# Layer 1's kept weights at the other end of SBUF, and SyncE's transfers of one pass in program order

## The chip, the cores and the metric

The kernel runs on one core of a Trainium2 chip. The metric is device time in microseconds: 1929.45 us before the change, the median of three runs (1929.41 to 1929.79). A core has five engines that run side by side [...]: TensorE (PE, matmuls), VectorE (DVE), ScalarE (ACT), GpSimd (POOL) and SyncE (SP). SyncE computes nothing here; it issues most of the transfers. GpSimd issues those whose rows are chosen by the data (indirect ones). [...]

## The reference, cut to what matters

Two layers, on 8192 tokens of 256 floats (128 graphs of 64 nodes). In each layer a graph part and then a part with experts is added to x:

```python
# layer 0
x = x + gnn0(layernorm(x), adj)          # silu(rmsnorm((adj @ h + eps*h) @ W1)) @ W2
x = x + ffn0(layernorm(x))               # 6 of 64 experts per token, each a 256x256 matrix, softmax weights;
                                         # the mix @ out_w, added to the input, layernorm (ln_g, ln_b)
# layer 1
x = x + gnn1(layernorm(x), adj)          # h = layernorm(.; gamma, beta); . + relu((adj @ h) @ W_rel + h @ W_root)
x = x + ffn1(layernorm(x))               # 2 of 8 experts per token: relu(x @ W1 + b1) @ W2 + b2, softmax weights
```

All of it is float32. The counts of tokens per expert are known only on the chip.

## The kernel before, in words

Tokens are worked on in NB = 32 blocks of C = 256 (T = 2 tiles of 128). There are four passes.

1. The first pass computes layer 0's graph part block by block, chooses six experts for each token, and has GpSimd scatter six copies of each row, with a destination row and a weight, into a table in DRAM that is sorted by expert (`r0x`; `Router.send`, L415).
2. The lattice pass (L1120 to L1222) reads that table in pages of 128 rows into `px` buffers, a ring of 31, multiplies each page by its expert's matrix in `lat` (128 KB of each partition of SBUF), weights the result in place, and has GpSimd scatter it back, one indirect transfer for each of 390 pages, into `r0y`, six rows per token (`Router.reply`, L424). At its end stands a branch (L1217) for pages that only an uneven choice of experts would need; it isn't taken in these runs. Where it isn't taken, each engine adds to the semaphores what its part of the branch would have added; GpSimd does so after waiting for all its earlier transfers.
3. The fused pass (L1348 to L1676) is the rest of layer 0 and layer 1's graph part and choice of experts. `load_y` (L1364) loads the six rows of each token of a block, `load3` (L1378) the residual x1 and the adjacency. `fold` (L1405, VectorE) adds two of the six rows to others from block 8 on, `mixture` (L1384) sums the rest with transposing matmuls, `out_proj` (L1396) applies out_w, `output` (L1414) the layernorm; `flip_h`, `neighbours`, `convolve_a` and `convolve_b` are layer 1's graph part with W_rel and W_root; `residual` (L1504) makes x3 and stores it; `flip3` (L1525) transposes it into `xn3T` by TensorE and a copy on ScalarE (L1529), and `gate1` (L1531) multiplies that by Wg. `choice`, `slots` and `send1` then place and scatter two copies of each row into a second table, `r1x`. Meanwhile `load_w2` (L1548) loads the eight W2 matrices of layer 1's experts into `fw2`, which is kept to the end.
4. The last pass works on pages of 256 rows of `r1x`: W1, relu, W2, and an accumulating scatter into the output. Its first four pages (-4 to -1) are fetched, and partly computed, in the fused pass's last stages (`fetch1`, L1252).

The order of the fused pass is written out by hand in the list at L1594: `staggered` runs stage s = -4, -3, -2 and so on, and an entry (lag, f) calls f for block s - lag. So in stage s there is load_y for block s + 4, load3 for s + 2, mixture for s + 2, out_proj for s + 1, output for s, the graph part for s - 1, residual, flip3 and gate1 for s - 2, choice, slots and the first row transfer for s - 3, and the rest of the rows and W2 for s - 4. Line 690 fixes this order on TensorE, VectorE and ScalarE. SyncE and GpSimd aren't in that list: a scheduler orders their instructions when the kernel is built.

Memory comes from pools. A pool is put at the lower end of what is free, or, with side="right", at the upper end. `lat` and above it `wx0`, with the `px` and `pxT` buffers, are freed before the fused pass; its pools then take the same bytes. With reuse_waits="tile" the first instruction that writes a tile waits for the last users of those earlier tiles whose bytes it takes, and for no others. In the kernel before, `keep` (fw2, 32 KB of each partition) takes the lower end of the old `lat`, then come `c3` (weights, adjacency) and `work3` (y, x1, xs, xn3T and the rest); `wx1` (layer 1's pages and W1) is at the upper end. `work3` ends at byte 174080; `lat` had ended at 154592, so that its last tiles (three of the four xs buffers and part of another, xn3T, the one-hot tiles) lie where pxT and px buffers were.

SyncE's transfers use eight completion semaphores in turn, so that at most eight are on their way: each waits for the one eight before it.

Of the kernel before, what the change touches and what calls it, by code (L numbers as in the profile page):

```python
# [9 lines left out]
F32 = mybir.dt.float32  # L10
# [3 lines left out]
ENG = mybir.EngineType  # L14
# [5 lines left out]
P = 128  # L20
# [637 lines left out]
def staggered(n, stages, first=0):  # L658

    for s in range(first + min(lag for lag, _ in stages), n + max(lag for lag, _ in stages)):  # L660
        for lag, f in stages:
            if first <= s - lag < n:
                f(s - lag)
# [3 lines left out]
def two_layer_gnn_moe_kernel(ctx: ExitStack, tc: tile.TileContext, a: dict, out: bass.AP):  # L667
    nc = tc.nc
    x_in, adjT = a["x"], a["adjT"]
    N, D = x_in.shape  # L670
# [3 lines left out]
    KD = D // P  # L674
# [7 lines left out]
    E1, F1, _ = a["L1_ffn_W2"].shape  # L682
# [34 lines left out]
    def load_matrix(pool, name, engine=nc.scalar):  # L717

        t = pool.tile([P, a[name].shape[0] // P, a[name].shape[1]], F32, name="m_" + name)
        engine.dma_start(out=t, in_=a[name].rearrange("(k p) f -> p k f", p=P))  # L720
        return t
# [20 lines left out]
    def clear_adjacency(pool, engine):  # L742
        for i in range(4):
            at = pool.tile([P, T, P], F32, name=f"at{i}")
            engine.memset(at, 0.0)
            adjacency.append(at)
# [31 lines left out]
    with tc.tile_pool(name="c0", bufs=1) as c0, \  # L778
# [290 lines left out]
        n = free[0] // 16  # L1069
# [153 lines left out]
    lat_pool.__exit__(None, None, None)  # L1223


    keep = ctx.enter_context(tc.tile_pool(name="keep", bufs=1, reuse_waits="tile"))
    fw1 = a["L1_ffn_W1b1"]
    F1W = fw1.shape[2]
    fw2 = keep.tile([P, E1, KF, D], F32, name="fw2")
# [66 lines left out]
    def bend(i, c0):  # L1296
        Q = pages[i]
        m = Q["n"] * P
        if c0 == 0:
            Q["hid"] = wx.tile([P, KF, PG], F32, name="phid")  # L1300
        for c in range(c0, c0 + Q["group"]):
            nc.scalar.activation(Q["hid"][:, c, :m], Q["up", c][:, :m], AF.Relu,  # L1302
                                 bias=Q["w"][:, KD * F1 + c:KD * F1 + c + 1], scale=1.0)

    def up(i):
        for c in range(0, KF, pages[i]["group"]):
            products(i, c)
            bend(i, c)
# [23 lines left out]
    def gather(i):  # L1332
        Q = pages[i]
        y, n = Q["x"], Q["n"]
        nc.vector.tensor_add(y[:, :n, :D], Q["py"][:, :n, :], Q["b2"].unsqueeze(1).to_broadcast([P, n, D]))  # L1335
# [12 lines left out]
    with tc.tile_pool(name="c3", bufs=1, reuse_waits="tile") as c3, \  # L1348
# [1 line left out]
            tc.tile_pool(name="ps3", bufs=3, space=PSUM, reuse_waits="tile") as psum, \  # L1350
            tc.tile_pool(name="po3", bufs=1, space=PSUM, reuse_waits="tile") as po_pool, \
            tc.tile_pool(name="pm3", bufs=1, space=PSUM, reuse_waits="tile") as pmix:
        out_wT = load_matrix(c3, "L0_ffn_out_wT")
        ln_g, ln_b, gamma, beta, bg = (over[x] for x in ("ln_g", "ln_b", "gamma", "beta", "bg"))
        w_rel, w_root = (c3.tile([P, KD, D], F32, name="m_" + x) for x in ("rel", "root"))
        wg = load_matrix(c3, "L1_ffn_Wg")
        clear_adjacency(c3, nc.vector)
        one = c3.tile([P, P], F32, name="one")
        nc.vector.memset(one, 1.0)
# [11 lines left out]
                    tc.declare_no_dep(d.ins, group="r0last", reason="in the first pages, or waited for above")  # L1371

        def load_weights(b):
            if b == 0:
                for t, v in ((w_rel, "L1_gnn_W_rel"), (w_root, "L1_gnn_W_root")):
                    nc.sync.dma_start(out=t, in_=a[v].rearrange("(k p) f -> p k f", p=P))

        def load3(b):  # L1378
# [90 lines left out]
        def flip_h(b):  # L1469

            B = blocks[b]
            pt = psum.tile([P, KD, C], F32, name="ps")
            ops.transpose(pt, B["hn"])
            B["hT"] = hT = work.tile([P, KD, C], F32, name="hT", bufs=1)
            for k in range(KD):
                nc.scalar.activation(hT[:, k, :], pt[:, k, :], AF.Identity, bias=beta[:, k:k + 1], scale=gamma[:, k:k + 1])
# [95 lines left out]
        def places_of(i):  # L1572
            def half(c):
                if c % 2 == 0:
                    pages[i]["two"] = (po_pool.tile([P, T, D], F32, name="po") if c % 4 == 2 else
                                       psum.tile([P, KD, C], F32, name="ps"))
                return pages[i]["two"][:, c % 2, :]

            pages[i].update(pt=lambda c: psum.tile([P, KD, C], F32, name="ps"), ph=half, group=2,
                            py=lambda c: po_pool.tile([P, T, D], F32, name=("pz", "pc")[i % 2]))  # L1580

        def ahead(*work):

            def do(b):
                for n, f in work:
                    if n == b - NB:
                        f()
            return do

        for i in (-4, -3, -2):  # L1590
            places_of(i)
        usual = NB - 2

        staggered(NB, (  # L1594
            (-2, load3),
            (-3, load_weights),
            (-4, load_y),
            (1, lambda b: flip_h(b) if b >= usual else None),
            (2, R),
            (0, A),  # L1600
# [64 lines left out]
            (4, load_w2),  # L1665
            (4, ahead((-3, lambda: bend(-3, 2)), (-3, lambda: gather(-4)))),
        ))
        r1.page_lists(work.tile([P, 512], F32, name="scratch", bufs=1))
        up(-2)
        down(-3, 1)  # L1670
# [85 lines left out]
```

## Time and profile before

| | |
|---|---|
| median of 3 runs | 1929.45 us (1929.41 to 1929.79) |
| the profiled execution | 1929.21 us, of which the span is 1927.4 us |
| TensorE, busy | 1831.9 us, 95% of the span |
| VectorE, ScalarE, GpSimd, busy | 1148.4, 1002.1, 1133.4 us |
| the branch at the lattice pass's end | 1063.7 us after the span's start |
| the fused pass's own matmuls | from 1072.9 to about 1443 us |
| granted clock of TensorE, mean | 0.978 |

All times in the text are microseconds from the start of the span of one profiled execution, unless they are called time of a run. A line of the timeline shows start, length, engine, source line, operation, output and inputs; in brackets the idle time before it and what ended that. A line of the waits shows who waited for whom: total, how often, and the longest. "SPq" and the like are the sequencers, where transfers are issued; a landing is seen only in who it lets go.

### The profile page before, as it was taken

The page shows a single profiled execution, that of the slowest core. Times are in us where ns is not written, and L with a number is a line of the kernel's source. Part 1 is how long each engine was busy: PE and PEld are TensorE (multiplying, and loading weights), DVE is VectorE, ACT ScalarE, POOL GpSimd, SP SyncE. Part 2 cuts the span into 40 slices and gives each one's busy share as a digit, 9 for nine tenths or more (in the row PEclk, how much of TensorE's full clock was granted, in tenths as well). Part 3 has the DMA queues.
Part 4 walks back from the last instruction along what each step waited for, and adds up shares of the span by engine and source line. Part 5 has one row for each costly group of instructions (what it writes and reads, how often), then busy time and mean ns, then how long its engine had stood idle before and what let it go on. Part 6 is the DMA issues. An engine that isn't in the chain of part 4 may idle for free. (4 is left out here: it accounts for less than half of the span.)

```text
span 1927.4 us, 35251 instructions
## 1 busy us (share of the span) xinstructions
PE 1831.9 (95%) x9906; PEld 1607.9 (83%) x9906; DVE 1148.4 (60%) x4260; ACT 1002.1 (52%) x2047; POOL 1133.4 (59%) x1114
## 2 busy tenths in 40 slices
PE   7999999999965999999999769999999999999997
PEld 6888888888854788888888668888888888888886
DVE  6899999999977343444434449999974222222221
ACT  5888989989861222222222336666663333333332
POOL 1277777777777777777777744444444544444443
PEclk9999999999987999999999889999999999999999
DMA  5244555454376999876666969978525765666653
GB/s 142 63 135 142 162 164 156 153 161 146 122 243 200 296 287 284 258 215 207 208 206 188 340 204 351 329 259 289 179 100 138 171 145 125 132 135 130 136 100 63
DMA packets 253086, 359.49 MB, mean 187 GB/s; under 512 B 53177, under 2 KB 210505, under 8 KB 252881
## 3 DMA queue, kind: packets, MB, share of 16 engines
q1 hardware_dynamic: 185120, 219.20, 38.7%
q0 software_dynamic: 62736, 135.21, 23.7%
q10 hardware_dynamic: 5024, 2.66, 0.5%
q8 instruction: 90, 1.47, 0.3%
q14 instruction: 116, 0.94, 0.2%
HBM read 193.27 MB, written 166.03 MB: 186 GB/s over the span
## 5 line engine op out<-in xcount | busy, mean ns | idle before, releaser
L419 POOL DMA_INDIRECT r0x<-xs,r0row x384 | 385.5, 1004 | 214.6 <-ACT lat L887 114.8
L426 POOL DMA_INDIRECT r0y<-px x390 | 379.6, 973 | 121.3 <-DMA r0y<-px 48.4
L1191 PE MATMUL py<-lat,pxT 128*128 x1616 | 381.4, 381 | 4.4 <-ACT pxT L1168 4.2
L436 POOL DMA_INDIRECT out_x<-px x131 | 203.0, 1550 | 265.7 <-DVE px L1341 182.5
L1195 DVE TENSOR_SCALAR px<-py,px 128x256 f32<-128x256 f32 x390 | 170.9, 480 | 271.5 <-PE py L1191 270.2
L1191 PEld LDWEIGHTS py<-lat,pxT 128*128 128x128 f32 x1616 | 293.3, 191 | 38.0 <-ACT pxT L1168 5.2
L1168 ACT COPY pxT<-pt 128x512 f32<-128x512 f32 x188 | 110.2, 588 | 318.0 <-PE pt L1165 284.2
L1302 ACT ACTIVATE phid<-ph,pw 128x256 f32<-128x256 f32 (+1 forms) x264 | 122.2, 463 | 287.9 <-PE ph L1293 180.8
L419 POOL DMA_INDIRECT r1x<-xs,r1row x128 | 135.7, 1060 | 174.9 <-ACT hn L1456 49.0
L898 PE MATMUL ps<-lat 128*128 128x256 f32 x1024 | 238.1, 381 | 0.0
L862 PE MATMUL ph<-lat 128*128 128x256 f32 x1024 | 231.9, 385 | 3.1 <-DVE lat L885 2.0
L1318 PE MATMUL py<-fw,phid 128*128 (+1 forms) x1016 | 230.4, 379 | 0.0
L1293 PE MATMUL ph<-pxT,pw 128*128 128x256 f32 (+1 forms) x1056 | 227.3, 368 | 1.5 <-DVE px L1335 1.5
L862 PEld LDWEIGHTS ph<-lat 128*128 128x128 f32 x1024 | 195.0, 193 | 29.7 <-issue 2.5
L898 PEld LDWEIGHTS ps<-lat 128*128 128x128 f32 x1024 | 192.9, 191 | 27.8
L1293 PEld LDWEIGHTS ph<-pxT,pw 128*128 128x128 f32 x1056 | 192.9, 190 | 26.6 <-DVE px L1335 1.9
L1318 PEld LDWEIGHTS py<-fw,phid 128*128 128x128 f32 x1016 | 187.9, 190 | 22.8
L1329 DVE TENSOR_SCALAR p<-p 128x2 f32<-128x2 f32 (+1 forms) x69 | 12.6, 183 | 207.9 <-ACT p L1328 207.9
L1335 DVE TENSOR_TENSOR px<-py,pb 128x512 f32<-128x512 f32 (+1 forms) x67 | 44.5, 664 | 138.5 <-PE py L1318 136.3
L885 DVE SCALAR_TENSOR_TENSOR lat<-ph,c_L_gnn_b,rms 128x256 f32<-128x256 f32 x256 | 111.9, 477 | 22.8 <-ACT rms L72 22.8
L865 ACT ACTIVATE lat<-ph,c_L_gnn_b 128x256 f32<-128x256 f32 x256 | 103.7, 471 | 32.2 <-PE ph L862 27.6
L1165 PE MATMUL pt<-ident,px 128*128 128x128 f32 x780 | 116.6, 273 | 3.9 <-DMA px<-r0x 3.9
(338 smaller groups left out, 2958.4 us busy)
## 6 DMA issues: line engine op xcount, KB each, us to landing
y<-r0y SPq DMA_DIRECT2D x64, 768.0 KB
px<-r0x SPq DMA_DIRECT2D x376, 129.0 KB
pw<-in_L_ffn_W1b SPq DMA_DIRECT2D x41, 514.0 KB
x<-x SPq DMA_DIRECT2D x64, 256.0 KB
px<-r1x SPq DMA_DIRECT2D x28, 516.0 KB
r0x<-r0filler SPq DMA_DIRECT2D x65, 129.0 KB
lat<-in_x SPq DMA_DIRECT2D x32, 256.0 KB
lat<-in_L_ffn_lattice_weights SPq DMA_DIRECT2D x8, 1024.0 KB
```

Source lines behind the costliest of these rows:

```text
L419: i = self.nc.gpsimd.indirect_dma_start(out=self.table[:, :], out_offset=bass.IndirectOffsetOnAxis(ap=row[:, t, k:k + 1], axis=0), in_=xs[ ...
L426: d = self.nc.gpsimd.indirect_dma_start(out=self.answer[:, :], out_offset=bass.IndirectOffsetOnAxis(ap=x[:, self.D:self.D + 1].bitcast(I32 ...
L436: i, d = f"{self.name}add{i}", self.nc.gpsimd.indirect_dma_start(out=self.total[:, :], out_offset=bass.IndirectOffsetOnAxis(ap=x[:, self.D ...
L862: nc.tensor.matmul(ph[:, c, :], lhsT=w1[:, k, ts(2 * j + c, P)], rhs=B["aggT"][:, k, :], start=(k == 0), stop=(k == KD - 1))
L885: nc.vector.scalar_tensor_tensor(hT[:, c, :], B["ph", c // 2][:, c % 2, :], b1[:, c:c + 1], B["rms"], op0=ALU.add, op1=ALU.mult)
L898: nc.tensor.matmul(B["po"][:, t, :], lhsT=B["hT"][:, c, ts(t, P)], rhs=w2[:, c, :], start=False, stop=(t == T - 1 and c == KH - 1))
L1165: nc.tensor.transpose(pt[:, k, ts(q, P)], Q["px"][:, q, ts(k, P)], ident)
L1191: nc.tensor.matmul(py[:, q, :], lhsT=xT[q][:, k, ts(h, P)] if parts == 2 else xT[:, k, ts(q, P)], rhs=lat[:, ds(e, 1), k, :].rearrange("p ...
L1195: nc.vector.tensor_scalar(px[:, q, :D], py[:, q, :], px[:, q, D + 1:D + 2], None, op0=ALU.mult)
L1293: nc.tensor.matmul(Q["up", c][:, :m], lhsT=Q["w"][:, k * F1 + c * P:k * F1 + (c + 1) * P], rhs=Q["xT"][:, k, :m], start=(k == 0), stop=(k ...
L1302: nc.scalar.activation(Q["hid"][:, c, :m], Q["up", c][:, :m], AF.Relu, bias=Q["w"][:, KD * F1 + c:KD * F1 + c + 1], scale=1.0)
L1318: nc.tensor.matmul(py[:, t, :], lhsT=Q["hid"][:, c, ts(t, P)], rhs=fw2[:, ds(e, 1), c, :].rearrange("p o d -> p (o d)"), start=(c == 0), s ...
```

## The change

Three things are edited. The pool `keep` is put at the upper end of the free memory, so that `wx1` comes below it, and `c3` and `work3` start where `keep` was. SyncE is put under the hand-written order for the length of the fused pass's loop. And the order itself is changed: load_y stands first in each stage, then the weights, then load3. The weights out_w and Wg, which ScalarE loaded ahead of the loop, are now loaded by SyncE within it, as W_rel and W_root were: out_w behind y of block 1, W_rel and W_root behind y of block 3, Wg behind y of block 4.

```diff
-    keep = ctx.enter_context(tc.tile_pool(name="keep", bufs=1, reuse_waits="tile"))
+    keep = ctx.enter_context(tc.tile_pool(name="keep", bufs=1, side="right", reuse_waits="tile"))
...
-        out_wT = load_matrix(c3, "L0_ffn_out_wT")
         ln_g, ln_b, gamma, beta, bg = (over[x] for x in ("ln_g", "ln_b", "gamma", "beta", "bg"))
         w_rel, w_root = (c3.tile([P, KD, D], F32, name="m_" + x) for x in ("rel", "root"))
-        wg = load_matrix(c3, "L1_ffn_Wg")
+        out_wT, wg = (c3.tile([P, KD, n], F32, name="m_" + x) for x, n in (("out", D), ("wg", E1)))
...
         def load_weights(b):
-            if b == 0:
-                for t, v in ((w_rel, "L1_gnn_W_rel"), (w_root, "L1_gnn_W_root")):
+            for n, t, v in ((1, out_wT, "L0_ffn_out_wT"), (3, w_rel, "L1_gnn_W_rel"), (3, w_root, "L1_gnn_W_root"),
+                            (4, wg, "L1_ffn_Wg")):
+                if b == n:
                     nc.sync.dma_start(out=t, in_=a[v].rearrange("(k p) f -> p k f", p=P))
...
+        in_order = tc.manual_schedule(engines={ENG.SP})
+        in_order.__enter__()
         usual = NB - 2
 
         staggered(NB, (
+            (-4, load_y),
+            (-4, load_weights),
             (-2, load3),
-            (-3, load_weights),
-            (-4, load_y),
...
         ))
+        in_order.__exit__(None, None, None)
         r1.page_lists(work.tile([P, 512], F32, name="scratch", bufs=1))
```

The orders that the two builds give, at the fused pass's start on SyncE (a number is the block; y(b) and each adjacency are two transfers):

```
before: rel root at0 y0 y1 x0 y2 x1 at1 y3 x2 at2 y4 x3 at3 y5 x4 at4 y6 out0 x5 at5 y7 ...   (out_w, Wg on ScalarE)
after:  y0 y1 out_w y2 x0 at0 y3 rel root x1 at1 y4 Wg x2 at2 y5 x3 at3 y6 x4 at4 out0 y7 x5 at5 ...
```

In the build after, `c3` and `work3` lie at bytes 23520 to 141312 of each partition, `wx1` at 147040 to 196576 and `fw2` at 196576 to 229344.

## The prediction

> **What bounds the kernel now.** I read the page first, then the fused pass in windows, then the list of waits there, then TensorE's and GpSimd's timelines and the chain around the two holes that the windows showed.
>
> ```profile
> span 1927.4 us, 35251 instructions
> PE 1831.9 (95%) x9906; PEld 1607.9 (83%) x9906; DVE 1148.4 (60%) x4260; ACT 1002.1 (52%) x2047; POOL 1133.4 (59%) x1114
> ```
>
> TensorE sets the time: 95% busy. What can be gained is where it stands still or runs slowly. Windows of the fused pass (length; busy us of PE, PEld, DVE, ACT, POOL; granted clock, DMA share, GB/s):
>
> ```profile
> 1063.00:1070.00 7.00, 0.00 (x0) 0.00 (x0) 1.51 (x8) 0.00 (x0) 5.17 (x7) 0.63 0.79 243
> 1080.00:1093.00 13.00, 10.35 (x71) 9.00 (x72) 8.59 (x30) 5.50 (x11) 10.11 (x10) 1.00 1.04 394
> 1093.00:1111.00 18.00, 17.84 (x105) 15.63 (x103) 9.21 (x36) 8.90 (x20) 13.69 (x14) 1.00 0.98 352
> 1111.00:1126.00 15.00, 0.00 (x0) 0.00 (x0) 3.59 (x12) 0.40 (x1) 9.71 (x10) 0.67 0.63 205
> 1126.00:1142.00 16.00, 15.76 (x87) 14.58 (x88) 5.97 (x33) 8.45 (x20) 2.04 (x5) 0.78 0.32 117
> 1142.00:1160.00 18.00, 18.00 (x120) 16.20 (x119) 15.39 (x79) 11.45 (x25) 8.11 (x9) 1.00 0.90 279
> ```
>
> Two holes: the start, with saturated DMA, and 1111 to 1126, where nothing but GpSimd works. From 1142 to the pass's end TensorE is full. The waits between 1063 and 1130 say who holds the second hole (total us, times, longest):
>
> ```profile
> ACT xn3T L1529 <- DMA r0y<-px: 16.9, 1, 16.9
> PE pg L1535 <- ACT xn3T L1529: 15.4, 1, 15.4
> ```
>
> ScalarE's first copy into xn3T waits for replies of the layer before, scattered from px buffers; the gate's matmul waits for the copy. In the program built from the kernel before, xn3T lies at bytes 169664 to 171712 of a partition, inside two px buffers; the copy must wait for replies, and for counts that GpSimd adds only after all its earlier scatters have landed. TensorE and GpSimd there:
>
> ```profile
> 1109.81 1.03 PE L1501 MATMUL pc<-z,at 128*128 128x256 f32 x4
> 1126.24 1.88 PE L1535 MATMUL pg<-m_L_ffn_Wg,xn3T 128*128 128x8 f32 x8 [15.40 <-ACT xn3T L1529]
> 1127.97 5.28 PE L1391 MATMUL ps<-ident,y 128*128 128x128 f32 x24
> 1133.08 0.60 PE L89 MATMUL ps<-ident,hn 128*128 128x128 f32 x4
> ...
> 1140.60 1.06 PE L1535 MATMUL pg<-m_L_ffn_Wg,xn3T 128*128 128x8 f32 x8
> 1141.52 2.82 PE L1391 MATMUL ps<-ident,y 128*128 128x128 f32 x24
> 1144.17 0.60 PE L89 MATMUL ps<-ident,hn 128*128 128x128 f32 x4
> ```
> ```profile
> 1122.60 0.97 POOL L426 DMA_INDIRECT r0y<-px  x1 [0.30 <-issue]
> 1126.23 0.97 POOL L426 DMA_INDIRECT r0y<-px  x1 [2.66 <-DMA r0y<-px]
> ```
>
> The reader sees the hole (15.40), and gate and transposes behind it taking about twice as long as one block later. For the first hole, the chain (start, length):
>
> ```profile
> 1080.25 12.14 DMA y<-r0y
> 1092.43 1.53 PE ps L1391 x12
> ```
>
> [...] The trace prices those two issues at 0.45 and 0.79 us, on a ScalarE then idle for 20 us.
>
> **The change, part by part.**
>
> 1. *The kept weights on the right.* In the new build, c3 and work3 take bytes 23520 to 141312, all inside the lattice weights (23520 to 154592), whose last reader is TensorE at 1062.3. The copy into xn3T has no wait for scatters left; neither have the one-hot tiles and the xs buffers that lay on px or pxT. The orders on TensorE, VectorE, ScalarE (but for its two issues) and GpSimd are unchanged. Worth: the idle 15.40; the gate from 1126.24 to 1127.97 (1.73) against 1140.60 to 1141.52 (0.92), 0.81; the transposes 1127.97 to 1133.08 (5.11) against 1141.52 to 1144.17 (2.65), 2.46. Together 18.7.
>
> 2. *Where the wait goes.* fw2 now lies on px (196576 to 229344). SyncE's first W2 load (L1550, stage 4) waits for the last scatter: 1126.23 + 0.97 and a landing of about 1.7 (1123.57 to 1125.29, where ScalarE was let go) gives 1129. SyncE gets there after the store of stage 4's start, 1142.1 before, about 1123 now: held 6 us. Behind it stand y(9), x1(7), the adjacency and later stores. y(9) would land at about 1129 + (512 + 1536 KB)/300 = 1136 (rate in 3); its fold is due near 1150. Cost 0, with 14 us of cover; without cover up to 6. GpSimd starts layer 1's rows after the last scatter and three dest writes (0.61): 1129 instead of 1141.5. Block 0 is sent by about 1135, landed by 1138; xs(4) reuses its buffer near 1148. Cost 0.
>
> 3. *The start.* Between 1080.25, when y(1) has landed, and 1092.39, when y(3) has, SP's row moves x1(0), y(2), x1(1), one adjacency, y(3): 256 + 1536 + 256 + 64 + 1536 = 3648 KB in 12.14 us, 300 KB/us, in issue order (SP's issue of x1(2), waiting for x1(0), stands at 1081.28). Before y(1) went rel, out, root, Wg, one adjacency: 840 KB, 2.8 us. So y(1) lands at 1077.4 and y(3), again 3648 KB later, at 1089.6. But x1(0) now stands behind y(2): 1077.4 + 2048/300 = 1084.2, and VectorE's output(0), at 1083.79 before, begins no earlier. rel, root and x1(1) stand behind y(3): x1(1) lands 768 KB later, 1092.2. output(1) began at 1089.69; now 1092.2. Its two adds, statistics and aggregates took 1.75 (1089.69 to 1091.44), then ScalarE's root 0.3, accT(3) 0.5, half of hT(0) 0.55, and 0.1 for the hand-overs: `neighbours(0)` can begin at 1095.4, where it began at 1096.17. Gain 0.8 at best; I take 0.5. Bounds: -2, if x1(0) or x1(1) lands later; +2.6, if x1(1) isn't late. y(4), 1600 KB after x1(1), lands at 1097.5 against a need at about 1100. out lands near 1078.3 (needed 1079), rel 1090.5 and root 1091.3 (needed 1095 and 1097), Wg after y(4) (needed 1110). All 0.
>
> 4. *SyncE's order later.* The cycle y, x1, adjacency, store is that of before; y(s+4) goes right after the store of stage s-1, 2.8 stages (28 us) before its fold, for a transfer of 5 to 8. Cost 0. Two things move: r1's second filler, hoisted to the kernel's beginning before, is now issued with `look`, and the column behind it must wait for that and for block 16's first row, which holds SyncE for most of a stage; y(24) then has about 16 us. And three W1 loads, made around stage 12 before, come in stages 28 to 30, with the first pages; flip1(-4) came at 1417.18, 27 us after the store of stage 28 (1389.70), for 900 KB, 3 us. Both 0, with at most one transfer (3 to 8 us) at stake.
>
> Sum: 18.7 + 0.5 = 19.2. Against the profiled execution: span 1927.4 to 1908.2; with the 1.8 around it (1929.21 - 1927.4), 1910.0. The median, 1929.45, stands 0.24 higher: 1910.2. What lies behind the pass is TensorE alone and shifts whole.
>
> **The rivals.**
>
> *A full start gain.* If transfers share the engines rather than follow in order, x1(1) isn't late and the start gives its 2.6: 1929.45 - 18.7 - 2.6 = 1908.2. Against it: x1(0)'s landing in order.
>
> *Part comes back.* GpSimd is 12 us ahead of its old place, TensorE 19; or x1 lands later; or SyncE's hold has less cover than I count. Any one gives 2 to 9 back: 1912.5 to 1919. For it: GpSimd starts 7 us late against stage 3. Against: 1.28 us a row, four a block, in stages of 11.
>
> *SyncE's hold becomes the bound; slower.* Place: L1550's first wait; price: one us of TensorE for each us that y(9) lands after 1150. It equals before when SyncE is let go at 1161, and makes 1934 at 1166. For it: strict order, everything behind one wait. Against: the last scatter has landed by 1129, and no scatter waits for the pass.
>
> *No change.* The copy's wait is gone but the gate stands as long for another, Wg or the branch on GpSimd. Against: in the new build, the gate waits for the copy and Wg only, which has 12 us.
>
> **How the numbers follow.** Forecast (1909 to 1912.5) 0.70; full start gain 0.10; part back 0.15; SyncE slower 0.03; no change 0.02. A measurement of this kernel can tell about 0.2%, 4 us, from no change: faster 0.70 + 0.10 + 0.15 = 0.95, same 0.02, slower 0.03. The range takes the forecast, the start's gain and 2 us below it for the bounds in 3, and most of what may come back: 1906 to 1916.5.
>
> **What would show it.** Right: no idle over 2 us on TensorE between 1100 and 1142; the wait xn3T on r0y gone; gate and transposes at 0.92 and 2.65 throughout; SyncE's longest new wait L1550 on r0y, 4 to 8 us, with nobody waiting for y after it; y(3)'s transposes near 1089.6, `neighbours(0)` near 1095.5. Wrong: VectorE waiting for y at L1412 or x1 at L1419 after 1100, ScalarE waiting for sends at L1521, or the 2.8 of the start kept in full.

## The result and the profile after

The changed kernel takes 1910.05 us (median of five runs, 1908.79 to 1911.01). The kernel before, run beside it, took 1929.79 (1929.41 to 1933.56). The ratio is 0.9893, with a 95% interval from 0.9879 to 0.9908; the forecast was 1910.2. The profiled execution took 1908.79 us, of which 1907.0 are the span.

The busy times of the changed kernel (its span is 1907.0 us), then its windows of the fused pass (columns as in the prediction's windows: length, busy us and count of PE, PEld, DVE, ACT, POOL, granted clock, DMA share, GB/s):

```profile
PE 1830.7 (96%) x9906; PEld 1605.9 (84%) x9906; DVE 1148.6 (60%) x4260; ACT 1002.4 (53%) x2047; POOL 1136.5 (60%) x1114
```
```profile
1080.00:1093.00 13.00, 9.11 (x65) 7.51 (x64) 6.77 (x23) 3.51 (x9) 9.96 (x11) 1.00 1.05 383
...
1111.00:1126.00 15.00, 15.00 (x105) 13.62 (x104) 12.40 (x64) 9.71 (x22) 11.02 (x11) 1.00 0.86 317
1126.00:1142.00 16.00, 16.00 (x104) 14.12 (x103) 12.17 (x65) 9.17 (x21) 9.34 (x13) 1.00 0.70 234
```

TensorE has the same number of matmuls and nearly the same busy time as before (1831.9). What went is idle time and slow matmuls: from 1111 to 1126, where TensorE had stood for the whole 15 us at a clock of 0.67, it is busy for 15.00 at 1.00, and the clock of 0.78 behind it is 1.00 too. The hole at the start is still there (9.11 of 13).

The waits of all engines between 1055 and 1160, and SyncE's own; xn3T no longer waits for r0y, and SyncE has a new wait at L1550:

```profile
ACT xn3T L1529 <- PE ps L89: 7.6, 5, 1.6
```
```profile
SPq L1550 <- DMA r0y<-px: 7.5, 2, 4.3
```

TensorE's timeline around the first gate, which answers the 15.40 us of before:

```profile
1109.32 1.03 PE L1535 MATMUL pg<-m_wg,xn3T 128*128 128x8 f32 x8
1110.21 2.82 PE L1391 MATMUL ps<-ident,y 128*128 128x128 f32 x24
1112.86 0.60 PE L89 MATMUL ps<-ident,hn 128*128 128x128 f32 x4
```

The gate has no idle time ahead of it; from its start to the transposes are 0.89 us (1.73 before), from there to the next 2.65 (5.11 before). `flip_h` of block 2 starts at 1112.86 and not at 1133.08, which is 20.22 earlier. This splits into three parts. TensorE's last product of layer 0 ended at 1061.35 and not at 1062.28: 0.93, which has nothing to do with the pass. From that product to `neighbours(0)` it took 33.34 (to 1094.69) and not 33.89 (to 1096.17): 0.55. The rest, 18.74, is the stall. The end of the span is 20.4 earlier.

Where the wait went, in SyncE's timeline and GpSimd's:

```profile
1121.90 0.55 SPq L1508 DMA_DIRECT2D out_x<-x  x1
1130.19 0.38 SPq L1550 DMA_DIRECT2D fw<-in_L_ffn_W  x1
```
```profile
1127.78 0.97 POOL L426 DMA_INDIRECT r0y<-px  x1 [2.67 <-DVE xs L370]
...
1129.57 1.04 POOL L419 DMA_INDIRECT r1x<-xs,r1row  x1 [0.17 <-POOL xs L366]
```

SyncE stands 7.7 us between the end of one issue (1122.45) and the next, until layer 0's last scatter, issued at 1127.78, has landed; y(9), which stands behind that wait, is issued at 1130.62. In the windows from 1111 to 1142 TensorE has no gap. Of the start, these are the chain's last two pieces in the hole (start, length), and TensorE's line at its end:

```profile
1082.26 9.25 DMA x<-x
1091.61 0.89 DVE h L1419 x2
```
```profile
1092.54 0.39 PE L1399 MATMUL po<-p_L_ffn_out_b,r0ones 128*128 128x512 bf16 x1 [1.87 <-DVE h L1419]
```

x1(1) is the last thing in the chain. `output(1)` starts when it has landed, and TensorE waits 1.87 us for `output(1)`.

### The profile page after: what moved, and what is told of

It reads as the page before. It is cut to its first block, busy times and chain, and to the rows that moved or that the text cites. A ratio compares the mean times of both kernels' runs of the same rounds, so it can differ in the third digit from the quotient of the medians.

```text
span 1907.0 us, 35224 instructions
## 1 busy us (share of the span) xinstructions
PE 1830.7 (96%) x9906; PEld 1605.9 (84%) x9906; DVE 1148.6 (60%) x4260; ACT 1002.4 (53%) x2047; POOL 1136.5 (60%) x1114
```

## The experiments

**Each half alone.** The theory says that the stall is a matter of the bytes that xn3T lies on, and that SyncE's order brings half a microsecond. So one kernel has the placement alone and one has the order alone.

```diff
 # e1: the kernel before, and
-    keep = ctx.enter_context(tc.tile_pool(name="keep", bufs=1, reuse_waits="tile"))
+    keep = ctx.enter_context(tc.tile_pool(name="keep", bufs=1, side="right", reuse_waits="tile"))
```

> The kernel before with one edit: the kept weights at SBUF's right end; SyncE's order stays the scheduler's, out and Wg stay on ScalarE's queue. Theory (the stall is a matter of where xn3T lies): the 15.4 us of TensorE's idle and the 3.3 us at a slow clock go, 18.7 us, so the median is near 1911 (1910 to 1911.8), at most 1.5 us from the changed kernel. TensorE has no idle of over 2 us between the start of the pass and its end, the gate of block 0 takes 0.92 and the 24 transposes behind it 2.65. Start: x1(1) stands ahead of y(3) here, so TensorE does not wait for output(1), but y(3) itself has 264 to 840 KB more ahead of it and is 1 to 2 us later. Rival (the program order of SyncE is needed for the gain, since an early load of W2 or a late y takes the stall's place): 1915 or more, with a wait of TensorE or VectorE on y or x1 after 1100 us.

```diff
 # e2: the changed kernel, and
-    keep = ctx.enter_context(tc.tile_pool(name="keep", bufs=1, side="right", reuse_waits="tile"))
+    keep = ctx.enter_context(tc.tile_pool(name="keep", bufs=1, reuse_waits="tile"))
```

> The changed kernel with one edit undone: the kept weights back at the left end, SyncE in program order. Theory: the copy into xn3T waits for GpSimd's last scatters again, which end near 1125 us whatever SyncE does, so the start gain is swallowed: 1929 (1928 to 1930.5), and TensorE's idle ahead of the gate is 15 to 17 us, longer by what the start has won. Rival (the order itself brings a part of the 19.4 us): 1910 plus 18.7 = 1928.7 at most if the order's 0.7 us add up, under 1927 if it brings more.

In one session with the kernel before at 1930.05, the placement alone took 1911.41 us (0.9901, 0.9886 to 0.9916) and the order alone 1930.36 (1.0001, 0.9992 to 1.0009). TensorE at the gate, first with the placement alone and then with the order alone:

```profile
1112.98 1.03 PE L1535 MATMUL pg<-m_L_ffn_Wg,xn3T 128*128 128x8 f32 x8
```
```profile
1127.64 1.88 PE L1535 MATMUL pg<-m_wg,xn3T 128*128 128x8 f32 x8 [15.58 <-ACT xn3T L1529]
1129.37 5.13 PE L1391 MATMUL ps<-ident,y 128*128 128x128 f32 x24
```

The placement carries the gain: 1930.05 - 1911.41 = 18.6 us, where the sum had 18.7. With the scheduler's own order SyncE is held by the same scatters (7.5 us at L1550), again at no cost, so program order is not a condition of the gain. The start went as expected for e1: TensorE doesn't wait for `output(1)` there, but 1.08 and 1.23 us for y(3), which comes late with more ahead of it. Expected wrongly was that no idle would be over 2 us: one of 2.14 stands ahead of y(1)'s transposes. The order alone brings nothing that can be told from zero: the idle of 15.58 and the slow matmuls of 1.88 and 5.13 are all back.

**One tile or the placement.** If the wait belongs to the bytes, taking xn3T alone out of the way must leave the wait to the next tile that lies on px.

```diff
 # e5: the kernel before, and
+        xn3T = c3.tile([P, KD, C], F32, name="xn3T")
...
-            blocks[b]["xn3T"] = xT = work.tile([P, KD, C], F32, name="xn3T", bufs=1)
+            blocks[b]["xn3T"] = xT = xn3T
```

> The kernel before with one edit: xn3T alone is taken from the pass's constants, at bytes 67104 to 69152, inside the lattice weights; all tiles of the work pool lie 2048 bytes higher. Theory (the wait belongs to the bytes, so the next tile on px takes it): VectorE's first one-hot tile of layer 1, two steps behind the gate, now waits until about 1125 us, holding VectorE's order; TensorE runs on for some 10 us to the first matmul of the positions, which reads the one-hot tile, and stands there 5 to 9 us, with slow matmuls behind it. Time 1915 to 1923, say 1918.5. Rival (xn3T alone was in the way): near 1911, like the changed kernel. Rival (any of the tiles costs the whole stall): 1928 to 1930.

It took 1924.9 us (0.9976, 0.9966 to 0.9985), 1.9 above the range that was expected; its profiled execution was the fastest, at 1920.84. VectorE's and TensorE's timelines (line numbers from the new line on are one higher):

```profile
1125.88 0.17 DVE L254 TENSOR_TENSOR r1hot<-r1tags,r1which 128x32 bf16<-128x32 bf16 x1 [10.87 <-DMA r0y<-px]
```
```profile
1126.11 0.20 PE L269 MATMUL pos<-r1hot,r0tri 128*128 128x16 bf16 x2 [8.01 <-DVE r1hot L254]
...
1128.58 1.91 PE L1502 MATMUL pc<-z,at 128*128 128x256 f32 x4
1130.28 1.71 PE L1536 MATMUL pg<-m_L_ffn_Wg,xn3T 128*128 128x8 f32 x8
1131.85 4.47 PE L1392 MATMUL ps<-ident,y 128*128 128x128 f32 x24
```

The one-hot tile takes the wait over, at the named place. TensorE gets 10 us further and then stands 8.01 us, plus 0.82 and 0.23 for xs behind it; the matmuls after that run slowly (1.91 for 1.03, 1.71 for 1.06, 4.47 for 2.82, and 0.74 on the four transposes of xs): 3.9 more. So 13.0 of the 18.7 us remain, and 5.7 would be won; the medians say 1930.05 - 1924.9 = 5.2. The mechanism was right; the expectation of 1918.5 counted too little for the slow matmuls and the hand-overs. Of the 4 us between the profiled execution and the median, 1.7 can be the earlier end of its layer 0 (1060.54 against 1062.28 before); a second profile (e9) fell into the session described next and says nothing, so the rest stays open.

**SyncE's hold.** The prediction gave it no cost, because y(9) has some 14 us to spare. If so, the same wait met two stages earlier must cost what y(7) comes late, and four stages later nothing may change.

```diff
 # e6, e10 (stage 2), e7 (stage 1), e8, e12 (stage 8): the changed kernel, and
-            (4, load_w2),
+            (2, load_w2),        # 1 in e7, 8 in e8 and e12
```

> The changed kernel with the loads of W2 at lag 2 in place of 4, so that SyncE meets its wait for layer 0's scatters two stages earlier, behind the store of stage 2. Theory (the wait is hidden only while y has cover): SyncE is held from about 1105 to 1130, 25 us in place of 7.7; y(7) stands behind it, lands about 1136.3 (256 + 1536 KB at 300 KB/us after 1130.2), its transposes are due at 1132: TensorE waits 4 to 5 us there, 1914.6 (1913 to 1917). Rival (the hold itself costs, whatever its place): the changed kernel has already lost something to it, and here it is three times as long: 1920 or more. Rival (free, since transfers catch up): 1910.

> The same at lag 1: SyncE is held from about 1099 to 1130, and y(6) and x1(4) stand behind it. Theory: y(6) lands at 1136.3 and was due at 1121.3; TensorE waits 15 us, and two to three us more go into slow matmuls behind the idle: 1925 to 1931, say 1928, most of the change's gain given back to a wait on another queue. Each us that a y lands after its transposes are due costs one. Rival (free): 1910; rival (half of it caught up elsewhere): 1918.

> The changed kernel with the loads of W2 at lag 8, from stage 8 on, when all scatters have long landed. Theory: SyncE's hold of 7.7 us is gone, y(9) is issued some 7 us earlier, and the time is the same, 1910 (1909 to 1911.2), because y(9) had over 10 us to spare. Rival (the hold costs a part of its 7.7): 1903 to 1908. Rival (16 loads of W2 later in the pass collide with the first pages): 1912 or more.

> The kernel with xn3T alone moved, a second time and a second profile, since the profiled execution (1920.84) was 4 us under the median of its timed ones (1924.9). If VectorE's wait at the one-hot tile sets the time, the idle of TensorE ahead of the positions' matmul is longer in the slower execution by about the difference; if it is 8 again in an execution of 1924 to 1926, the 4 us lie elsewhere.

In that session every kernel took about 345 us longer, the kernel before too (2274.85), so its times are no evidence on the hold. It ran on another chip than the sessions before and after it, so whether the chip or the moment made it slow can't be told. The figures are: e6 2276.31 (1.0006, 0.9983 to 1.0028), e7 2273.98 (0.9998, 0.9967 to 1.0028), e8 2275.4 (1.0014, 0.999 to 1.0038), and a single execution of e9, 2288.53. Layer 0 had grown; the largest of TensorE's waits in it were for ScalarE's copies (82.3 and 75.6 us in e6), and what slowed those was not found. GpSimd's last reply, in e6:

```profile
1445.51 0.97 POOL L426 DMA_INDIRECT r0y<-px  x1 [6.70 <-DMA r0y<-px]
```

TensorE's last product of layer 0 had ended at 1436.6, 9 us before. In the changed kernel at its usual length the last reply comes 66 us after it (1127.78 against 1061.35). In e6 SyncE doesn't stand at L1550: its first load there is issued at 1472.6, 27 us after that reply. And three versions of the changed pass take the time of the kernel before (0.9998 to 1.0014). So in these runs the gain came with a backlog on GpSimd (19.7 us where the last reply was 66 us behind TensorE, none where it was 9); how it grows with the backlog was not measured.

Stages 2 and 8 were run again, stage 1 was not: what a y that is 15 us late costs stays unmeasured.

> The changed kernel with the loads of W2 at lag 2 in place of 4, as in e6, whose session says nothing on it: layer 0 took 370 us longer there, so that GpSimd had kept up and its last scatters had landed before SyncE came to W2. Here, with layer 0 at its usual length: theory, SyncE is held from about 1105 to 1130, y(7) lands about 1136.3 and was due at 1132: TensorE waits 4 to 5 us, 1914.6 (1913 to 1917). Rival (the hold itself costs, whatever its place): 1920 or more. Rival (free): 1910.

> The changed kernel with the loads of W2 at lag 8, as in e8, whose session says nothing on it. Theory (the 7.7 us of SyncE's hold are hidden, y(9) having over 10 us to spare): the same time as the changed kernel beside it within 1.2 us. Rival (the hold costs a part of its 7.7): 2 to 7 us less. Rival (later loads of W2 collide with the first pages): 2 us more or worse.

At stage 2: 1917.02 us (0.9933, 0.9919 to 0.9946), 7.0 more than the changed kernel's 1910.05, or 6.1 if each is set against the kernel before beside it (1930.62 here). SyncE's waits and TensorE's timeline:

```profile
SPq L1550 <- DMA r0y<-px: 25.2, 2, 22.1
```
```profile
1135.21 2.59 PE L1391 MATMUL ps<-ident,y 128*128 128x128 f32 x12 [3.05 <-DMA y<-r0y]
1138.55 2.82 PE L1391 MATMUL ps<-ident,y 128*128 128x128 f32 x12 [0.75 <-DMA y<-r0y]
1141.16 1.06 PE L89 MATMUL ps<-ident,hn 128*128 128x128 f32 x4
```

y(7) comes 3.8 us late, near the 4 to 5 expected from 1792 KB at 300 KB/us. But the 24 transposes take 2.59 + 2.82 where they took 2.82, and those of hn 1.06 for 0.60: 3.05 more, since TensorE is slow again. 3.8 + 3.05 = 6.85, near the 6.1 to 7.0 measured. So in these runs the hold became the bound only where a y was late, and there the slow matmuls came on top of the lateness. Their part didn't grow with the stall: 3.05 here behind 3.8 us of idle, 3.9 in e5 behind 9.1, 3.3 in the kernel before behind 15.4. At stage 8, beside the changed kernel on one chip: 1911.16 (0.9903, 0.9887 to 0.992) against 1910.02. L1550 no longer waits for r0y, and y(9) is issued at 1123.80, not at 1132.69 as beside it. 8.9 us earlier bring nothing (1.1 us more, in runs that overlap): the hold was hidden.

**The start.** The profile after names x1(1) as the last to land, with W_rel and W_root ahead of it. Changing two lines over puts them behind it.

```diff
 # e3, e13: the changed kernel, and
             (-4, load_y),
-            (-4, load_weights),
             (-2, load3),
+            (-4, load_weights),
```

> The changed kernel with two lines of the pass's list changed over: x1 and the adjacency ahead of the stage's weights, so that x1(1) is issued ahead of rel and root, and x1(2) ahead of Wg. Theory (transfers of SyncE land in the order of issue at about 300 KB/us): x1(1) has 512 KB less ahead of it and lands 1.7 us earlier, output(1) no longer starts late, TensorE's idle of 1.87 us ahead of out_proj(2) falls to under 0.3, and the kernel takes 1.6 to 1.9 us less than the changed one: near 1908.3. rel lands about 1091 and root 1092, still ahead of neighbours(0) at about 1093. Rival (transfers in flight share the engines, so that the order of two of them says little): the same 1910, idle still 1.5 to 1.9. Second rival (rel or root is now the late one): neighbours(0) waits for m_rel, gain under 1.

> The changed kernel unaltered, on the chip of the two beside it, so that differences of 1 to 2 us can be read without the kernel before in between: 1910 (1908.8 to 1911.2), 0.9885 to 0.9905 of the kernel before.

> As e3 (x1 ahead of rel, root and Wg), beside the changed kernel on one chip. Theory: 1.0 to 1.9 us less than it, since the idle of 1.87 ahead of out_proj(2) goes and y(3) comes half a us later; rival: the same, the 1.9 us between the medians of two sessions being chance.

e3 took 1908.18 us (0.9885, 0.987 to 0.99), 1.9 under the changed kernel of the other session. Side by side, the changed kernel took 1910.02 (0.9896, 0.9879 to 0.9912) and the new order 1907.56 (0.9889, 0.9872 to 0.9905), 2.5 less; their runs spread over 1.7 and 4.4 us and overlap. Of all eight runs of the new order, e3 and e13, seven lie under the fastest of the nine of the changed kernel (1908.79). The traces say where. TensorE in e13:

```profile
1088.74 0.55 PE L89 MATMUL ps<-ident,hn 128*128 128x128 f32 x3 [0.16 <-ACT hn L1456]
1089.22 0.39 PE L1399 MATMUL po<-p_L_ffn_out_b,r0ones 128*128 128x512 bf16 x1
```

The idle ahead of out_proj(2), 1.87 to 2.54 in all five profiles with the change's own order, is gone in both of these. From y(3)'s last transposes to `neighbours(0)` it is 6.3 to 7.9 us in the five, and 4.3 and 4.5 in the two. The time from TensorE's last product of layer 0 to `neighbours(0)`, in us:

| SyncE's order | profiles | mean |
|---|---|---|
| before (before, e5) | 33.89, 33.31 | 33.6 |
| the scheduler's with the placement (e1) | 34.33 | 34.3 |
| the change's (after, e2, e10, e11, e12) | 33.34, 32.24, 33.78, 34.02, 33.38 | 33.35 |
| x1 ahead of the weights (e3, e13) | 32.45, 30.56 | 31.5 |

The change's order wins 0.25 by these means, with a scatter of 1.8 between profiles, so its sign isn't certain. It brings y(3)'s last transposes 3.6 us earlier (26.2 us after the last product of layer 0, against 29.9, in the mean), and the late x1(1) takes nearly all of that back. x1 ahead of the weights wins some 1.8 more. This order is the fastest version that was run.

## Why the prediction was right

**Step 1, the placement: right, with its size.** 18.7 was forecast from idle 15.40, gate 0.81 and transposes 2.46. The traces give 18.74, and the placement alone 18.6. The waits listed as gone beside xn3T's, of the one-hot tiles and of xs, had to go as well: e5 shows that they alone would have kept 13.0 of the 18.7.

**Step 2, where the wait goes: right.** SyncE stood at L1550 for 7.7 us, forecast 6 (4 to 8), mostly because the last scatter was issued at 1127.78 and not at 1126.23; the rest is that SyncE got there half a microsecond earlier. GpSimd's layer-1 rows began at 1129.57, forecast 1129. Both cost nothing, and e12 shows it for SyncE. The rival in which SyncE's hold becomes the bound did not happen, but e10 shows that it is real two stages earlier, and that its price was too low: it was put at one us for each us that y is late, without the some 3 us of slow matmuls that e10 adds. By this figure its break-even, SyncE let go at 1161, would have come some 3 us earlier; that is an estimate.

**Step 3, the start: the path right, one branch of it left out, the closeness of the size luck.** y(3)'s last transposes came at 1088.42, forecast 1089.6, or 1088.7 counted from the earlier end of layer 0. That out_w and Wg land at the same 300 KB/us from SyncE's queue as from ScalarE's was the author's estimate: no run moves these two loads alone. x1(1) was late, as forecast, and the path ran as written, from `output(1)` through its statistics, ScalarE's root and accT to hT:

```profile
1093.40 0.30 ACT L36 ACTIVATE bn_sd<-bn_mv,eps 128x2 f32<-128x2 f32 x1 [2.35 <-DVE bn_mv L59]
1094.07 1.02 ACT L1476 ACTIVATE hT<-ps,r0delta,r0endrow 128x256 f32<-128x256 f32 x2
1094.69 2.02 PE L1484 MATMUL pz<-m_rel,hT 128*128 128x256 f32 x8
```
```profile
PEld pz L1484 <- ACT hT L1476: 0.6, 2, 0.4
```

`neighbours(0)` began 3.08 us after `output(1)`, forecast 3.2, and the weight load of its first matmul (PEld) waited 0.4 for hT. What the prediction left out is a second branch from the same `output(1)`: TensorE stood 1.87 us at out_proj(2), because that matmul writes the one `po` buffer that `output(1)` has yet to read. At the pace of the blocks before, 1.73 us, its eight matmuls were over at 1094.50, 0.2 before hT let TensorE go, so this branch cost nothing here. In e10, e11 and e12, where the matmuls behind that idle were slow, it was the longer one: `neighbours(0)` began 4.0 to 4.5 us after `output(1)`. That 0.55 us of gain agrees with the forecast of 0.5 is luck: the five profiles with this order scatter over 1.8, and their mean gain is 0.25. Both branches start at x1(1), whose lateness the prediction names, so e3's order, two lines away, could have been tried from the start.

**Step 4, SyncE later in the pass: right.** Of the filler's hold the wait list of the changed kernel shows 7.3 + 2.7 us at the line that reads the column, and 2.4 before a W1 load. From 1142 to the end TensorE waits for no y, x1 or page: its longest wait is 1.5, for VectorE.

**The sum.** Forecast 19.2; the medians give 1929.79 - 1910.05 = 19.7 beside each other, and 1929.97 - 1910.02 = 20.0 in the later session. The half microsecond above the forecast is within the scatter of layer 0's end, which moved by up to 4.5 us between profiles (1060.5 to 1065.0).

## What to carry to other kernels

The wait that came from reused memory belonged to bytes: with xn3T alone moved, the one-hot tile, which lies on px too, waited 10.87 us (e5). So list every tile that lies on them, not only the one that shows in the waits. Moving the pool that is written latest onto the memory that came free latest removed the wait for all of them at once (18.6 us, e1). What is then behind the late writer in its queue must have more cover than the wait is long: a hold of 7.7 us in stage 4 cost nothing, one of 25.5 us in stage 2 (e10) cost 6.1 to 7.0. The cover is worth measuring by moving the wait towards the start. In a stretch limited by transfers (DMA share 1.05 from 1080 to 1093, TensorE busy 9.11 of 13 us), order each queue by when its data is needed: x1(1), 256 KB that came late, held TensorE for 1.87 us.

## What the runs showed of the hardware that was not expected

TensorE's slow stretches also came behind gaps much shorter than the hole of 15.40 us. In e10 a gap of 3.05 us was followed by twelve transposes in 2.59 us, where twelve took 1.53 earlier in the same run (at 1079.97). At the start of the pass, after several gaps of 0.23 to 1.09 us, a gap of 1.89 to 2.05 was followed by slow matmuls in three profiles (e10, e11, e12; eight of out_proj in 3.57, 3.09 and 3.13 us) and one of 1.87 or 2.54 was not in two (after, e2; 1.89 us each). e11 shows it:

```profile
1093.31 0.39 PE L1399 MATMUL po<-p_L_ffn_out_b,r0ones 128*128 128x512 bf16 x1 [1.89 <-DVE h L1419]
1093.54 3.09 PE L1402 MATMUL po<-m_out,accT 128*128 128x256 f32 x8
1096.42 2.42 PE L1484 MATMUL pz<-m_rel,hT 128*128 128x256 f32 x8
```

The eight matmuls take 3.09 for 1.89, and the next eight 2.42 for 1.89: 1.7 us. So for gaps of 1.87 to 2.54 us it varied from one execution to the next whether slow matmuls followed. The length of the slow stretch is a matter of measurement too. The clocks of 0.67 and 0.78 in the prediction's windows are means: in the hole of the kernel before, the clock was 1.00 until 1115 and 0.98 from there to 1116, some 5 us after the last matmul, then 0.50, and it stayed at 0.50 for 6.8 us of work (1126.2 to 1133.0). Matmuls were slow for about as long in e2 (1127.64 to 1134.33) and in e10's second stall (1135.21 to 1142.02); behind the short gaps of e10, e11 and e12 they cost 1.7 us each, about half of the 3.3 of the kernel before. The sum did not suffer, since its slow matmuls were read from the lines.

The other surprise is the session in which layer 0 took 1436 and not 1061 us with the same instructions, and three versions of the change were worth nothing (0.9998 to 1.0014): what the removal of the wait for GpSimd brought depended on GpSimd still lagging, by 66 us in the changed kernel and by 9 in e6.
